# A macaron block on one core: x + y/2 scattered beside each row of f and added in its leaf tile

## The chip, the core and the metric

The kernel runs on one core of one Trainium2 chip. A core has a matrix engine (TensorE, PE in the profile; PEld is its weight load), a vector engine (VectorE, DVE), a scalar engine (ScalarE, ACT), a general engine (GpSimd, POOL) and a synchronising engine (SyncE, SP). Transfers between the core's memory (SBUF) and the chip's memory (DRAM) are issued from the queues of SP, ACT and POOL; those with a list of row numbers (indirect ones) are issued from POOL. PE's results land in a small memory of its own (PSUM, eight banks).

The metric is the time of one execution in microseconds (us) on the device, as the median of several runs. The profile comes from one profiled execution of the same program; its span reaches from its first to its last instruction.

## The reference

x has 4 x 1024 tokens of 256 values. The function does three steps; each adds to x:

```
x = x + 0.5 * ffn(layernorm(x))
x = x + attn(layernorm(x))          # 16 heads, latent k and v, rotation, masked by pages of 64
x = x + 0.5 * ffn(layernorm(x))
```

with the same ffn both times:

```
xn  = (x - mean) / sqrt(std + 1e-5)
q, k, v = tree_q(xn), tree_k(xn), tree_v(xn)             # relu inside
y   = xn + softmax(q k^T / sqrt(256)) v                  # over the 1024 tokens of a sequence
out = y + tree_f(y)                                      # gelu inside
```

A tree routes each token through eight levels of yes/no decisions (255 nodes) to one of 256 leaves. The leaf is a small two-layer network of its own: 256 to 16 values, an activation, 16 to 256.

So the second half of a step is x + 0.5 * (y + tree_f(y)), for every token.

## The kernel before

The 4096 tokens are 32 tiles of 128 (NT = 32). `xn` in SBUF holds a row of 256 values for each token, and in a 257th column, for the f tree, the token's number. `ffn` (line 1010) is called twice, with `attention` (line 1433) between; the text calls the two calls the first and the second pass.

A pass has these stages. First the norms and the routing of q, k and v. The tokens of a tree are sorted by groups of leaves into slots of 128-row tiles (at most 63 tiles, NGRP, of which mostly 48 to 53 are used), and `leaves` (line 810) runs the network of one such tile after another. Then comes the softmax stage: 32 steps, one for each tile of tokens. In step s, `begin_weights` transposes the exponentials of the tile before (PE L1001, copied out of PSUM by DVE and ACT at L1002), `score` makes the new scores (PE L978), their maximum (DVE L986) and the exponential (ACT L991), and `weigh` multiplies with v (PE L1006) and adds into `xn` (DVE L1008). That row of `xn` is now y. In the last eight steps the routing of f runs beside it (`route`: PE L389, L397, L409, DVE L405 and L417, POOL L419), then counting and ranking (`in_runs`, PE L455, L466, L467, L502, DVE L457 to L499), and the scatter of the rows of y to their slots in the DRAM buffer `xs_f` (`scatter`, POOL L691). Slots that get no token keep a row of zeros with a number that is out of bounds, written earlier by `clear` (ACT's queue, L329).

All of that stage stands in an order written out by hand: inside `in_order()` the engines PE, DVE, ACT and POOL run their instructions exactly as the program lists them. `at(step, where, do, ...)` puts a piece of work into a step: `where` 0 is ahead of the step's scores, 1 is between the scores' maximum and the exponential (and ahead of the routing's next piece), 2 is at the step's end. SP's queue takes its transfers in the order of the program, each waiting for what it depends on.

Then `leaves` runs for f. For each tile, SP loads 128 rows of `xs_f` (L820), PE transposes and multiplies them, DVE makes the masks, and at the end DVE adds the tile's rows of y to the result (L919), and POOL scatters the sum by token number into the DRAM buffer `ytok` (L920). The loads run four tiles ahead. Tiles past 48 run in branches of their own (`spare_leaves`). Beside the leaves, `reload` brings the pass's input x back into `xn` (SP, L128 in the first pass and L1380 in the second), as `xn` is no longer needed for y.

What follows needs x + 0.5 * ytok. `arrive` (line 1423) loads a piece of `ytok` (L1427) and adds it to `xn` (DVE L1429). After the first pass the attention calls it tile by tile as it begins, after a run of filler matmuls on PE (L144); it then takes the moments (bn_stats, L337), the layernorm (L1568), the latent and q, k, v matmuls (L1575, L1583, L1589) and the rotation (DVE L1486, L1488, POOL L1491), and transposes the result (L1499). After the second pass an end stage calls `arrive` for eight groups of four tiles (GT = 4) and stores each group into the output (ACT's queue, L1416).

In the pool `raw` two buffers with the tag "raw" take the f tree's first weights as they are loaded (`load_part`); their last use is in step 23.

## Time and profile before

| | |
|---|---|
| median of 11 runs | 2476.49 us (2473.18 to 2483.84) |
| the profiled execution's own time | 2478.45 us |
| its span | 2476.7 us |
| PE, DVE, ACT, POOL busy | 89%, 58%, 44%, 33% of the span |
| mean granted clock of PE | 0.945 |
| softmax stage, steps 26 to 31, second pass | about 2274 to 2337 us |
| 24 scatters of y rows without a gap, second pass | 2288.75 to 2319.1 us |
| f leaves, second pass | about 2355 to 2445 us |
| end stage | 2448.5 to 2476.7 us |
| opening of the attention | about 834 to 860 us |

The timeline lists instructions in order of time: start, length, engine, line and operation, tiles written and read, and in brackets how long the engine was idle before and what ended that. Lines like "x8" are several instructions in a row. The chain that ended last follows the work back from the last instruction, each step to what released it. The windows give, for a stretch, its length, the busy time of PE, PEld, DVE, ACT and POOL (with the number of instructions), PE's granted clock, the share of the DMA engines' time and the GB/s moved.

### The profile page before, as it was taken

The numbers are of one execution on the slowest core, as the hardware profiler recorded it, in microseconds if no ns is written. First come the engines' busy times: TensorE is split into PE (matmuls) and PEld (weight loads), VectorE is DVE, ScalarE is ACT, GpSimd is POOL, SyncE is SP. The second block draws the span as 40 slices with busy tenths as digits, with TensorE's granted clock in tenths as the row PEclk, the third lists the DMA queues.
The fourth block names the chain that finished last, engine by engine and source line by source line (L and its number), as shares of the span: only waits on it lengthen the run. The fifth ranks groups of instructions, "written<-read, shape, count | busy, mean of one in ns | idle before, by whom it ended". The sixth has DMA issues, their size and how long they took to land. (4 is left out here: it accounts for less than half of the span.)

```text
span 2476.7 us, 43530 instructions
## 1 busy us (share of the span) xinstructions
PE 2193.9 (89%) x14205; PEld 1419.1 (57%) x14205; DVE 1441.7 (58%) x4744; ACT 1096.9 (44%) x2902; POOL 818.4 (33%) x1053
## 2 busy tenths in 40 slices
PE   4498988999988899999999999985889989999794
PEld 2387866676657644334344434334778866766483
DVE  6676744333356766666676667745757543334475
ACT  3255655233214225555555555553556552332142
POOL 4554555343255421101101100002545663431553
PEclk8699999999998889999999999998999999999997
DMA  9667665343165300000000000017667553531655
GB/s 328 194 221 237 175 180 146 117 140 122 42 196 156 117 1 1 1 1 1 1 18 1 1 14 14 10 60 265 186 176 222 163 166 105 153 115 37 201 163 164
DMA packets 201877, 285.42 MB, mean 115 GB/s; under 512 B 25129, under 2 KB 174522, under 8 KB 197536
## 3 DMA queue, kind: packets, MB, share of 16 engines
q1 hardware_dynamic: 105232, 112.83, 14.1%
q0 software_dynamic: 35552, 91.87, 13.2%
q10 hardware_dynamic: 60848, 77.62, 9.6%
q8 instruction: 132, 2.16, 0.4%
q14 instruction: 113, 0.93, 0.1%
HBM read 182.75 MB, written 104.32 MB: 116 GB/s over the span
## 5 line engine op out<-in xcount | busy, mean ns | idle before, releaser
L1622 DVE TENSOR_REDUCE mxh<-big 128x1 f32<-128x512 f32 (+3 forms) x768 | 393.3, 552 | 194.1 <-PE big L1614 191.9
L1658 ACT ACTIVATE pTh<-big 128x512 f32<-128x512 f32 (+3 forms) x768 | 341.1, 491 | 288.9 <-PE big L1614 264.6
L1614 PE MATMUL big<-kTh,qTh 32*128 32x512 f32 (+3 forms) x1536 | 401.6, 539 | 1.3 <-ACT kTh L1595 1.2
L1650 PE MATMUL big<-qTh,kTh 32*128 32x512 f32 (+3 forms) x1536 | 399.8, 536 | 1.9 <-ACT pTh L1658 1.6
L829 ACT COPY xgT<-sm 128x256 f32<-128x256 f32 x399 | 148.4, 373 | 285.7 <-PE sm L827 255.5
L978 PE MATMUL two<-kT,qT 128*128 128x512 f32 x512 | 234.8, 603 | 10.2 <-issue 8.6
L1650 PEld LDWEIGHTS big<-qTh,kTh 32*128 32x128 f32 x1536 | 143.6, 184 | 156.3 <-issue 126.7
L1006 PE MATMUL sm<-vb,pT 128*128 128x256 f32 x1024 | 232.6, 380 | 0.0
L1006 PEld LDWEIGHTS sm<-vb,pT 128*128 128x128 f32 x1024 | 189.8, 190 | 24.7 <-issue 1.0
L827 PE MATMUL sm<-ident,xg 128*128 128x128 f32 x774 | 156.3, 286 | 42.9 <-DMA xg<-rows_x,inv_v 14.4
L986 DVE TENSOR_REDUCE mx<-two 128x1 f32<-128x1024 f32 x64 | 78.3, 1224 | 195.8 <-PE two L978 195.8
L865 DVE SCALAR_TENSOR_TENSOR went<-sm,sides 128x14 bf16<-128x14 f32 x399 | 68.3, 171 | 171.7 <-PE sm L856 162.1
L1669 PE MATMUL sm<-pTh,vpad 128*32 128x512 f32 (+3 forms) x1536 | 165.0, 501 | 0.0
L1614 PEld LDWEIGHTS big<-kTh,qTh 32*128 32x128 f32 x1536 | 146.6, 185 | 20.1 <-issue 14.2
L978 PEld LDWEIGHTS two<-kT,qT 128*128 128x128 f32 x512 | 94.1, 193 | 107.9 <-issue 103.1
L929 ACT COPY og<-sm 128x256 f32<-128x256 f32 x298 | 111.0, 373 | 79.5 <-DMA os_q<-og 16.0
L802 POOL DMA_INDIRECT xg<-rows_x,inv_q x101 | 101.2, 1002 | 114.0 <-PE sm L895 51.2
L920 POOL DMA_INDIRECT ytok<-og,tok x101 | 99.3, 983 | 80.4 <-DVE went L865 69.3
L419 POOL TENSOR_TENSOR acc<-acc,oh 128x32 bf16<-128x32 bf16 (+1 forms) x128 | 41.4, 323 | 252.5 <-DVE oh L417 216.0
L880 DVE TENSOR_TENSOR hm<-sm,mask 128x128 f32<-128x128 f32 x399 | 115.3, 289 | 10.0
L903 ACT ACTIVATE hid<-sm 128x128 f32<-128x128 f32 x399 | 112.9, 283 | 12.4 <-PE sm L895 11.8
L827 PEld LDWEIGHTS sm<-ident,xg 128*128 128x128 f32 x774 | 83.1, 148 | 60.9 <-issue 16.3
(367 smaller groups left out, 4541.9 us busy)
## 6 DMA issues: line engine op xcount, KB each, us to landing
xs_f<-zero ACTq DMA_DIRECT2D x14, 1028.0 KB
xg<-xs_f SPq DMA_DIRECT2D x101, 128.5 KB
os_q<-og SPq DMA_DIRECT2D x101, 128.0 KB
os_v<-og SPq DMA_DIRECT2D x101, 128.0 KB
os_k<-og SPq DMA_DIRECT2D x96, 128.0 KB
xn<-in_x SPq DMA_DIRECT2D x16, 512.0 KB
raw_q<-in_q_w SPq DMA_DIRECT2D x8, 1024.0 KB
w_q<-in_q_w SPq DMA_DIRECT2D x2, 4096.0 KB
```

The costliest lines, as they stand in the source:

```text
L827: nc.tensor.transpose(pa[:, c, :], xg[:, c * P : (c + 1) * P], ident)
L829: nc.scalar.copy(xT, pa)
L880: nc.vector.tensor_tensor(hm.rearrange("p (e l) -> p e l", l=LW), ph[:, :P].rearrange(split, l=LW), bc(mask[:, 0], 2, LW), ALU.mult,)
L903: nc.scalar.activation(hid, pt[:, 0], func)
L929: nc.scalar.copy(og, po)
L978: nc.tensor.matmul(ps[:, n0 : n0 + 512], qT[:, c, i * P : (i + 1) * P], kT[:, c, n0 : n0 + 512], start=(c == 0), stop=(c == KC - 1),)
L1006: nc.tensor.matmul(po, pT[:, j, :], vb[:, j, :], start=(j == 0), stop=(j == TPB - 1))
L1614: matmul = nc.tensor.matmul(ps[:, :n], qT[r : r + HPAD, hg, i * P : (i + 1) * P], kT[r : r + HPAD, hg, n0 : n0 + n], start=True, stop=True,)
L1622: nc.vector.tensor_reduce(maxima(b, hg)[:, i, c, u : u + 1], ps[:, :n], AX.X, ALU.max)
L1650: matmul = nc.tensor.matmul(ps[:, off:], kT[r : r + HPAD, hg, j * P : (j + 1) * P], qT[r : r + HPAD, hg, qb * QN + off : (qb + 1) * QN], s ...
L1658: nc.scalar.activation(pT[:, u, off:], ps[:, off:], AF.Exp, scale=1.0 / math.sqrt(HD))
L1669: nc.tensor.matmul(acc[r : r + HPAD, off:], vpads[b % 2][:, j, 4 * hg + 2 * pair + u, :], pTs[pair][:, u, off:], start=(j == 0), stop=(j = ...
```

## The change

A row of `xs_f` becomes 2 x 256 + 1 values wide: y, the token's number, and x + y/2. These rows are put together in SBUF, in buffers of four tiles (`sums[c]`, c from 0 to 7): `rest_of(c)` loads x (from the input, or in the second pass from `xrd`) into the last 256 columns, and `whole(t)` adds half of y to them on DVE and copies y and the number on ACT. The buffers share the tag "raw" with the weights for even c, and have a tag "sum" for odd c, two buffers each, so that group c takes the buffer of group c - 4. `scatter` then writes whole rows. In the order by hand, groups 0 to 3 are loaded in steps 24 and 25 and put together in step 26, groups 4 and 5 are loaded at the end of step 27 and put together in step 28, groups 6 and 7 are loaded at the end of step 28 and put together in step 30 and after the loop.

In the leaves, the first 257 columns are loaded as before, and the last 256 in a transfer of their own (`xs`). The result is 0.5 times the leaf's output plus `xs`, and is scattered by token into the output in the second pass, and in the first into `xmid`, from which the attention loads straight into `xn`. `reload`, the addition in `arrive` and the end stage are gone. In the first pass `clear` also zeroes the new columns, as a transfer of its own.

```diff
-    xs_f = dram.tile([NSLOT, E + 1], F32, name="xs_f")
-    ytok = dram.tile([NTOK, E], F32, name="ytok")
+    XSW = 2 * E + 1
+    xs_f = dram.tile([NSLOT, XSW], F32, name="xs_f")
+    xmid = dram.tile([NTOK, E], F32, name="xmid")
...
-    def scatter(slot, rows, views, *ts):
+    def scatter(slot, rows, views, sums, *ts):
...
-                in_=xn[:, t, :],
+                in_=sums[t // GT][:, t % GT],
...
-        raw = pool.tile([P, P, LW], F32, name=f"raw_{FFFS[f]}{hf}{c}", tag="raw", bufs=bufs)
+        size = GT * XSW if f == 3 else P * LW
+        raw = pool.tile([P, size], F32, name=f"raw_{FFFS[f]}{hf}{c}", tag="raw", bufs=bufs)
+        raw = raw[:, : P * LW].rearrange("p (e l) -> p e l", l=LW)
...
-                nc.sync.dma_start(xg, xs_f[g * P : (g + 1) * P, :])
+                nc.sync.dma_start(xg, xs_f[g * P : (g + 1) * P, : E + 1])
...
                 nc.vector.tensor_copy(tok, xg[:, E:])
-                kept[g] = tok, xg
+                xs = pool.tile([P, E], F32, name="xs", tag="xs", bufs=6)
+                nc.sync.dma_start(xs, xs_f[g * P : (g + 1) * P, E + 1 :])
+                kept[g] = tok, xs
...
-                tok, xg = kept.pop(g)
-                nc.vector.tensor_tensor(og, po, xg[:, :E], ALU.add)
+                tok, xs = kept.pop(g)
+                nc.vector.scalar_tensor_tensor(og, po, 0.5, xs, ALU.mult, ALU.add)
...
+                sums = {}
+
+                def rest_of(c):
+
+                    lo = c * GT
+                    sums[c] = raw.tile([P, GT, XSW], F32, name=f"sum{c}", tag=("raw", "sum")[c % 2], bufs=2)
+                    rows = (
+                        a["x"][lo // TPB, lo % TPB * P : (lo % TPB + GT) * P, :] if first
+                        else xrd[lo * P : (lo + GT) * P]
+                    )
+                    nc.sync.dma_start(
+                        sums[c][:, :, E + 1 :], rows.rearrange("(i p) e -> p i e", p=P)
+                    )
+
+                def whole(t):
+
+                    row = sums[t // GT][:, t % GT]
+                    nc.vector.scalar_tensor_tensor(
+                        row[:, E + 1 :], xn[:, t, :E], 0.5, row[:, E + 1 :], ALU.mult, ALU.add
+                    )
+                    nc.scalar.copy(row[:, : E + 1], xn[:, t, :])
...
-                    clear(nc.scalar, xs_f[k * 8 * P : min((k + 1) * 8 * P, NSLOT)])
+                    rows = slice(k * 8 * P, min((k + 1) * 8 * P, NSLOT))
+                    clear(nc.scalar, xs_f[rows, : E + 1])
+                    if first:
+                        clear(nc.scalar, xs_f[rows, E + 1 :])
...
                 at(26, 2, place_run, 0, 1)
                 at(27, 0, place_run, 0, 2)
+                for c in range(4):
+                    at(24 + c // 2, c % 2, rest_of, c)
+                    for t in range(c * GT, (c + 1) * GT):
+                        at(26, c % 2 + 1 - c // 2, whole, t)
                 for step in range(27, 30):
                     t = 8 * (step - 27)
                     for where, ts in enumerate((range(t, t + 2), range(t + 2, t + 5), range(t + 5, t + 8))):
                         at(step, where, go, *ts)
+                    if step < 29:
+                        for c in range(2 * step - 50, 2 * step - 48):
+                            at(step, 2, rest_of, c)
+                            for t in range(c * GT, min((c + 1) * GT, RUNS[1])):
+                                at(step + 1, c % 2, whole, t)
+                for t in range(24, 30):
+                    at(30, 1 + t // 28, whole, t)
                 for step, where in ((28, 0), (28, 1), (29, 0), (29, 1)):
                     at(step, where, place_run, 0, 1)
...
                 place_run(1, 9)
+                for t in range(30, NT):
+                    whole(t)
                 path = route(rp, (3,), NT - 1, *hot_f, 1)
...
-            def reload():
...
-                    places = dram_disjoint_views(ytok, NGRP)
+                    places = dram_disjoint_views(
+                        out.rearrange("b t e -> (b t) e") if last else xmid, NGRP
+                    )
...
-                    with_steps(leaves(*what), (1, reload()))
+                    drain(leaves(*what))
...
-            if last:
-                with ExitStack() as fs:
-                    ep = stage(fs, "end", 3)
-                    for c in range(NT // GT):
-                        ts_ = slice(c * GT, (c + 1) * GT)
-                        drain(arrive(ep, c * GT, (c + 1) * GT, nc.sync))
-                        nc.scalar.dma_start(
...
-    def arrive(pool, lo, hi, queue, tag="y", bufs=None):
...
+    def arrive(lo, hi, queue):
+
+        queue.dma_start(
+            xn[:, lo:hi, :E], xmid[lo * P : hi * P, :].rearrange("(i p) e -> p i e", p=P)
+        )
         yield
-        nc.vector.scalar_tensor_tensor(
-            xn[:, ts_, :E], y, 0.5, xn[:, ts_, :E], ALU.mult, ALU.add
-        )
```

## The prediction

> **What bounds the kernel now.** I read the chain that ended last, then the two places the change works in (the softmax stage before the f leaves, the opening of the middle attention), by timeline and by windows.
>
> The chain that ended last (start, length, what; us):
>
> ```profile
> 2444.15 4.34 DMA ytok<-og,tok
> ...
> 2449.32 4.52 DMA y<-ytok
> ...
> 2471.03 1.23 DVE xn L1429
> ```
>
> See: the last result scatter has landed at 2448.49. Everything after it, up to the span's end at 2476.70, is the end stage: eight loads of ytok, an addition each, eight stores.
>
> The softmax stage of the second pass, timeline, engine by engine (start, length, engine, line; idle before it in brackets):
>
> ```profile
> 2278.24 1.23 DVE L986 TENSOR_REDUCE mx<-two 128x1 f32<-128x1024 f32 x1 [3.13 <-PE two L978]
> 2279.57 0.28 DVE L417 TENSOR_TENSOR oh<-sm,rights 128x128 bf16<-128x128 f32 x1
> ...
> 2284.23 0.69 DVE L1002 COPY pT<-sm 128x512 f32<-128x512 f32 x1
> ...
> 2288.44 1.22 DVE L986 TENSOR_REDUCE mx<-two 128x1 f32<-128x1024 f32 x1
> ```
>
> ```profile
> 2282.10 0.18 PE L455 MATMUL sm<-acc,ones 128*128 128x32 bf16 x1
> ...
> 2291.20 1.09 PE L1001 MATMUL sm<-ident,pr 128*128 128x128 f32 x8 [0.23 <-ACT pr L991]
> ...
> 2296.18 0.17 PE L502 MATMUL sm<-upto,tri 32*32 32x1 bf16 x1
> ...
> 2299.84 1.04 PE L1001 MATMUL sm<-ident,pr 128*128 128x128 f32 x8
> ...
> 2320.41 0.18 PE L455 MATMUL sm<-acc,ones 128*128 128x32 bf16 x1 [1.31 <-POOL acc L419]
> ```
>
> See: PE is the bound and hardly idles. DVE has idle holes of 3 us, but it runs in written order, and in step 27 (2282.3 to 2291.0) there is no hole: the reduction at 2288.44 follows the ranks at once, and PE already waits 0.23 us for the exponential behind it. POOL issues 24 scatters without a gap from 2288.75 to 2319.1, one per 1.275 us; PE's 1.31 us wait at L455 is for POOL's sum behind them.
>
> PE clock (windows: length, busy of PE, PEld, DVE, ACT, POOL, PEclk):
>
> ```profile
> 850.00:851.00 1.00, 0.00 (x0) 0.00 (x0) 1.00 (x4) 0.00 (x0) 0.00 (x0) 1.00 0.00 0
> 851.00:852.00 1.00, 0.00 (x0) 0.00 (x0) 0.69 (x4) 0.00 (x0) 0.65 (x1) 0.57 0.00 0
> 852.00:853.00 1.00, 0.87 (x4) 0.71 (x4) 0.89 (x4) 0.00 (x0) 0.08 (x1) 0.50 0.00 0
> ```
>
> See: after about 2 us of idle PE the clock fell to half here. After the longer idle before the second pass's leaves it stayed at 0.50 from 2355 to about 2360.
>
> **The change part by part.** All is set against the profiled execution: span 2476.70, its time 2478.45.
>
> *End stage gone.* The span then ends shortly after 2448.49. I allow 0.5 us for the close: 2476.70 - 2449.0 = **-27.7** (bounds -26.5 to -28.2).
>
> *Opening of the attention.* The 17 additions at L1429 vanish, and bn_stats reads what the DMA brought. PE's first real matmul follows the filler at 845.7 and stays there. Then DVE's order counts: the q rotation (L1486) ran at 850.45 behind an addition of 1.20 us, though its matmuls (L1583) ended at 848.16; ACT's latent copy ran at 848.39, held by a factor that DVE gave late. Freed of them, rotation and both transposes behind it come 2.2 us earlier. Later additions (853.26, 859.57) may give a little more: **-3** (from -0.5, if another engine holds the chain, to -6, if the clock dip above also goes).
>
> *Whole rows made early.* Per pass 32 DVE operations of 128x256 with an immediate scalar: L1429's single-tile form took 426 ns, about 455 from start to start. 32 ACT copies: between 373 ns (L829, from PSUM) and 589 ns (L1117, SBUF to SBUF with scale and bias). ACT is 26% busy here (24.92 of the 97 us from 2240); in step 26 twelve copies, even of 589, leave the exponential done at 2284.9, just when the delayed PE comes for it. Cost nothing; without that cover the four of step 28 cost 2.4.
>  - Step 26, middle slot: eight of them (3.6 us) stand between the reduction and L417. L417 moves to 2283.2, POOL's sum behind it (0.44 us later, 1.21 long) ends at 2284.85, and PE's L455 runs at 2284.9 instead of 2282.10: +2.8. L1001 and the whole next step are queued behind it.
>  - Step 26, last slot: L457 to L662 (1.5 us, from 2285.1), then four more (1.8): the pT copy at 2288.4 instead of 2284.23. From that copy to the reduction it is 4.2 us with no hole: 2292.6 instead of 2288.44. With no slack behind it, **+4.2** in all so far.
>  - Step 28, first slot: four more, on rows that are loaded into the buffer that scatters 0 to 3 read. Scatter 3 ended on POOL at 2293.60, now 2297.8. Landing: the last xs_f scatter's POOL span ended at 2351.09 and the loads behind it were issued at 2352.93, so 1.84; in the first pass 2.0. Twice the bytes: bounds +0 and +1.0 (one more scatter's worth at the 130 GB/s or so of these stretches), I take +0.3. Then SP issues the 512 KB load: the first y load took 3.5 us to its addition (2448.89 to 2452.39); beside scatters a reload issued at 2295.30 still moved data until 2299.9, some 4.7 to 5.7 with its receipt. I take 4.3: there at 2304.5. DVE is ready at 2296.8 and waits 7.7. Then 1.8 for the four, 0.2 casts, 0.9 for the small chain to `upto`: PE's L502, in order ahead of L1006, runs at 2307.4 instead of 2296.18: **+11.2** in all. Both the exponential (reduction 2307.4) and step 29 sit behind.
>  - PE idles some 7 us there, so it resumes at half clock, as after 2355: 4.8 us at 0.5 lose **2.4**: +13.6. The 1.3 us wait at L455 (2320.41) is used up: **+12.3**.
>  - POOL: scatters 8 and 10 start after DVE's delayed casts (group 5's load lands at 2309.6, its four end at 2311.4), so the run of 24 ends 10.2 later, 2.1 ahead of PE. Step 30's six fit into DVE's holes of 2.2 (before L1008) and 1.0 us (before L457).
>
> Bounds per pass: 8.6 (landing 1.84, load 3.5, no clock loss) to 14.4 (landing 3, load 5.7). A second clock loss, for the 2.8 us wait of step 26, is left out: the dip at 851 came in a string of waits, here one stands alone. Two passes: **+24.6**.
>
> The Trainium skill, "TensorE: Matmul & The Clock Gate", Part 1, says that the clock halves after an idle window of about 3.4 us and returns after about as long a busy one: a rule against this change, which puts a 7 us hole into a stage that had none. By its figure the hole costs an estimated 1.7 in place of 2.4 and the whole sum would be 1.4 lower; the row above it, half clock after some 2 us of idle, is stricter than the rule.
>
> *Scatters with 2052-byte rows.* No row of the trace has them. POOL's time lies between 0.97 us (same 128 rows; a plain POOL load with 512 rows took only 0.82 to issue, so bytes and row count move it little) and 1.94 (proportional to bytes). I take 0.97, the nearer row.
>
> *Handover to the leaves.* Rows 30 and 31 put 0.9 us of DVE before L405, where it idled 0.79: +0.1. The last four scatters come after the 4 MB weights have gone by (350 GB/s until 2347), so their double size costs only its landing, +0.3 to +0.5. **+0.6** per pass (0 to 2), **+1.2**.
>
> *Leaves.* Steady tile: 1.507 us (L919 from 819.63 to 821.13), DVE busy 1.44 with a hole of 0.11. The new og form lies between 0.42 (L919) and 0.485 (L1008, pointer scalar): covered by the hole. If not, 0.06 x 50 = 3 per pass. 101 loads of xs (0.32 us of SP each) replace 16 reloads; SP has 1.2 us free per tile, xg buffers free earlier, and DMA share is 0.55. Nothing.
>
> *Clears.* Eight more of 1 MB in the first pass, on ACT's queue (0.37 us issue each) in steps with DMA at 0.40: nothing, at most +2 by late gathers.
>
> Sum: -27.7 - 3 + 24.6 + 1.2 = **-4.9**, 2473.55 against 2478.45. The median of the runs shown, 2476.49, is 1.96 below the profiled one: **2471.6**.
>
> **The rivals.**
>  1. *The holes hold it.* The rows arrive in time or DVE's waits fall beside PE work; only step 26's order costs (4.2 - 1.3 per pass). For: DVE is 44% busy in this stage. Against: the load cannot start before scatter 3 has landed, one slot ahead of its reader. -27.7 - 3 + 5.8 + 1.2 = -23.7: 2453.
>  2. *Longer rows cost POOL* (slower). The 24 + 4 scatters of a pass stand in a row on POOL; e more for each adds 56 e over both passes, less 4 (POOL ends 2.1 ahead of PE per pass). It turns to a loss at e = 0.16 us, over 0.2% from 0.25; at 0.3 it gives 2484, at 0.97 2522. For: POOL writes these DMAs itself, and no row of this length is measured. Against: the 512-row load above.
>  3. *A deeper wait* (even or slower). The loads of groups 4 and 5 share the queues with scatters of 262 KB each 1.275 us (206 GB/s) and take 4 to 7 us longer, per pass: 2480 to 2486. For: the queues peaked at 446 GB/s in such a load, so 190 to 240 are left. Against: 512 KB at 190 are 2.8 us, inside my 4.3.
>
> **How the numbers follow.** A measurement of this kernel can tell about 0.2% (5 us) from no change. Forecast case 0.58: its bounds run from -17 (-28.2 - 6 + 17.2) to +6 (-26.5 - 0.5 + 28.8 + 4), 2459 to 2482; 0.32 of it below -5, 0.22 within, 0.04 above. Rival 1 0.20, all faster. Rival 2 0.12: 0.02 within, 0.10 slower. Rival 3 0.10: 0.03 and 0.07. Faster 0.52, same 0.27, slower 0.21. The range leaves out the lower half of rival 1 and the upper parts of 2 and 3: 2453 to 2484.
>
> **What would show it.** No y or out loads after the last scatter; span ending about 0.5 us after its landing. In the second softmax stage: L455 of step 26 waiting about 2.8 us for POOL's sum; L502 of step 28 waiting about 7 us, with DVE stopped by the load of the recycled rows, then PEclk 0.5; 24 scatters with two gaps, each still 0.97. The attention's q rotation at about 3 us after the first real matmul instead of 4.7. I am wrong if the DVE wait in step 28 is under 3 us (rival 1), if a scatter takes over 1.1 us on POOL (rival 2), or if leaves take longer than 1.51 us a tile.

## The result, and the profile after

| | before | changed |
|---|---|---|
| median | 2476.49 us | 2536.13 us (2528.92 to 2541.59, 8 runs) |
| ratio, with its 95% interval | | 1.0238 (1.0224 to 1.0251) |
| the profiled execution's own time | 2478.45 us | 2522.99 us |
| its span | 2476.7 us | 2521.1 us |
| mean granted clock of PE | 0.945 | 0.943 |

The change makes the kernel 2.4% slower. The forecast was 2471.6 us with a range up to 2484, and 0.21 for slower.

Line numbers after the change are a little higher: the routing's sum is L420, its matmul L456, the small chain's matmul L503, the scores' exponential L996, the transposes L1006, the weights' matmul L1011, the fetch of q and k L1196, the rows' addition on DVE L1250 and copy on ACT L1253, the result's addition L924.

The stages can be set against each other by events that both traces have: the start of DVE's reduction (the scores' maximum) in each step of a softmax stage, the first and the last scatter of a result, and so on. In us:

| stretch | before | changed | difference |
|---|---|---|---|
| start to step 0, first pass (q, k, v) | 439.2 | 433.7 | -5.6 |
| first pass, steps 8 to 24 | 151.2 | 182.1 | **+30.9** |
| first pass, steps 26 to 31 | 48.5 | 64.2 | **+15.7** |
| first pass, step 31 to the first f result | 37.7 | 39.6 | +2.0 |
| first pass, f leaves | 71.1 | 71.1 | +0.1 |
| last f result to the attention's 48th maximum | 102.2 | 100.9 | -1.2 |
| second pass, steps 0 to 26 | 233.5 | 237.6 | +4.1 |
| second pass, steps 26 to 31 | 48.6 | 63.8 | **+15.2** |
| second pass, step 31 to the first f result | 37.3 | 39.2 | +1.9 |
| second pass, f leaves | 80.1 | 81.0 | +1.0 |
| last scatter to the end of the span | 32.5 | 13.2 | **-19.3** |

With -0.2 from the stretches not shown these make, but for rounding, +44.5, the difference of the spans. This profiled execution of the changed kernel is one of its quick ones, 13 us under its median. A second one, from the run `after_again` below, has a span of 2535.8; there the first row is -0.8, steps 8 to 24 +28.2, steps 26 to 31 +20.9 and +15.7. So the -5.6 in front, where nothing was changed, is scatter between executions and no part of the effect (in the runs below that start as fast, this stretch takes 436.0 to 443.9 us).

**The softmax stage of the first pass.** PE's waits of 3.9 to 7.6 us on rows of k that are fetched from DRAM by slot, timeline of the changed kernel:

```profile
509.56 0.41 PE L1196 MATMUL sm<-ident,y_k 128*128 128x128 f32 x2 [3.85 <-DMA y_k<-os_k,slot_k]
552.33 0.66 PE L1196 MATMUL sm<-ident,y_k 128*128 128x128 f32 x2 [7.62 <-DMA y_k<-os_k,slot_k]
600.52 0.66 PE L1196 MATMUL sm<-ident,y_k 128*128 128x128 f32 x2 [4.22 <-DMA y_k<-os_k,slot_k]
643.29 0.66 PE L1196 MATMUL sm<-ident,y_k 128*128 128x128 f32 x2 [6.37 <-DMA y_k<-os_k,slot_k]
```

These four make 22.1 us. After each of them the trace's records of the clock show it at half for 3.0 to 6.0 us of work, 16.6 us in all, which is an estimated 8 us more; the two together are 30 of the 30.9 us. The sum of these waits over the whole kernel, from the list of PE's waits, before and after (total, times, longest):

```profile
PE sm L1191 <- DMA y_k<-os_k,slot_k: 0.9, 1, 0.9
```

```profile
PE sm L1196 <- DMA y_k<-os_k,slot_k: 26.4, 8, 7.6
```

Windows of the same part of the stage (columns as ahead of the prediction; the last two are the DMA share and GB/s), before and after:

```profile
556.00:576.00 20.00, 20.00 (x91) 12.94 (x90) 7.09 (x13) 5.92 (x11) 1.99 (x6) 1.00 0.35 114
596.00:616.00 20.00, 20.00 (x91) 12.89 (x90) 7.09 (x13) 5.92 (x11) 3.87 (x8) 1.00 0.21 69
```

```profile
556.00:576.00 20.00, 20.00 (x93) 13.49 (x92) 6.89 (x12) 6.89 (x13) 3.81 (x4) 1.00 0.63 120
596.00:616.00 20.00, 15.78 (x68) 12.19 (x67) 5.07 (x9) 6.21 (x12) 5.79 (x7) 0.83 0.67 163
```

The first pair is the one to look at: the queues moved 120 GB/s instead of 114, but were busy 0.63 of the time instead of 0.35. The transfers had become slower, not only more. The records of single transfers say which. A clear's packets of 1028 bytes took 53 ns in the mean before; after the change those of 1028 bytes took 78 and those of 1024 bytes 103, with the same median (48 and 53) and a long tail. One clear lasted 3.3 to 5.4 us before, the pair of a step 11 to 16 us after, longer than a step of 9.4 us, and a fetch that is issued in that time shares the queues with it. In the second pass no byte is added to the clears, yet their packets rose from 52 to 80 ns: there only the distance between rows is new.

**Steps 26 to 31**, second pass, changed kernel, timeline of PE and then of DVE:

```profile
2329.66 0.18 PE L456 MATMUL sm<-acc,ones 128*128 128x32 bf16 x1 [1.68 <-POOL acc L420]
...
2339.72 1.09 PE L1006 MATMUL sm<-ident,pr 128*128 128x128 f32 x8 [1.13 <-ACT pr L996]
...
2353.56 0.18 PE L503 MATMUL sm<-upto,tri 32*32 32x1 bf16 x1 [8.79 <-DVE total L499]
2353.67 5.62 PE L1011 MATMUL sm<-vb,pT 128*128 128x256 f32 x16
...
2379.10 0.18 PE L456 MATMUL sm<-acc,ones 128*128 128x32 bf16 x1 [0.71 <-POOL acc L420]
...
2381.77 0.16 PE L488 MATMUL sm<-ones,acc 128*32 128x1 bf16 x1 [1.50 <-DVE cnt L458]
```

```profile
2325.29 2.77 DVE L1250 SCALAR_TENSOR_TENSOR sum<-xn,sum 128x256 f32<-128x256 f32 x8
...
2351.37 1.43 DVE L1250 SCALAR_TENSOR_TENSOR sum<-xn,sum 128x256 f32<-128x256 f32 x4 [10.27 <-DMA sum<-xrd]
...
2357.54 1.44 DVE L1250 SCALAR_TENSOR_TENSOR sum<-xn,sum 128x256 f32<-128x256 f32 x4 [2.48 <-DMA sum<-xrd]
...
2380.86 0.76 DVE L1250 SCALAR_TENSOR_TENSOR sum<-xn,sum 128x256 f32<-128x256 f32 x2 [1.95 <-DMA xs_f<-sum,slot_f]
```

Both waits of the prediction are there, in their places: the eight additions ahead of the routing in step 26 (PE waits for POOL's sum), and DVE's stop at the rows that are loaded into a buffer that scatters still read, with PE's small chain (L503) behind it and the weights' matmul at 5.62 us instead of 3.72. Before, that matmul was

```profile
2296.28 3.72 PE L1006 MATMUL sm<-vb,pT 128*128 128x256 f32 x16
```

A third wait is new: in step 30 (from 2374.58) DVE stops again, at the last two recycled rows that it makes there, and PE's L488 waits behind it. Counted from step 26's maximum (2278.24 before, 2323.96 after), PE's events come later by 1.8 us at the first routing sum (L455, now L456), by 11.7 at the small chain of step 28 (L503), by 13.0 at the second routing sum and by 15.2 at the small chain of step 30 (2387.60). So the second of DVE's waits, 2.48 us, cost nothing of its own, and step 30 cost 2.2 us. In the first pass of `after_again` step 30's wait is 6.43 us long, and that step takes 18.1 us instead of 11.5, which is what its +20.9 has over +15.7.

The clock around that stop, windows of 1 us:

```profile
2347.00:2348.00 1.00, 0.00 (x0) 0.00 (x0) 0.00 (x0) 0.57 (x3) 0.73 (x1) 0.65 1.15 45
2348.00:2349.00 1.00, 0.00 (x0) 0.00 (x0) 0.00 (x0) 0.00 (x0) 0.00 (x0) 0.50 0.68 171
...
2356.00:2357.00 1.00, 1.00 (x4) 0.82 (x3) 0.00 (x0) 0.30 (x2) 0.00 (x0) 0.50 1.12 416
2357.00:2358.00 1.00, 1.00 (x5) 0.86 (x4) 0.46 (x2) 0.00 (x0) 0.00 (x0) 0.73 0.92 357
```

PE's last work ended at 2344.77. A mean of 0.65 in the window from 2347 is 0.3 us at full and 0.7 at half clock, so the clock fell about 2.5 us after PE had stopped, and by the same reckoning it came back at about 2357.5, 4.0 us after PE had started again. The Trainium skill, "TensorE: Matmul & The Clock Gate", Part 1, gives about 3.4 us for both; here the fall came earlier and the return later. One wait gives no threshold, though. At the four waits for y_k above, the fall came 3.4 to 5.2 us after PE had stopped and the return 3.0 to 6.0 us after it had started again, and at a wait of 3.87 us in `after_again` (it ended at 514.33) the clock did not fall at all. In every trace here all stretches at half clock, but for those cut off by its end, last whole multiples of 3.41 us, so it matters where in this grid a wait falls.

**The end.** The chain that ended last is now one piece:

```profile
2507.95 0.98 DMA out<-og,tok
```

It started 13.2 us before the end of the span. What fills those is not in the views of the profile, since they leave out semaphore and queue work; the trace's own records have it (start, ns, engine, instruction, line):

```
2507.945   984  POOL  DMA_INDIRECT  out<-og,tok  L925
...
2512.540  7745  POOL  DRAIN  L1883
```

Between the two stands an instruction of 2054 ns on POOL, `INC_SWDGE_SEM`; the two together are called POOL's close here. SP was through by 2513.1 and waits for POOL until 2520.3. The same DRAIN of 7745 ns is in the trace of before, at 2448.74, where the end stage's loads and stores ran beside it.

### The profile page after: what moved, and what is told of

The parts are those of the page before. It is cut to its first block, busy times and chain, and to the rows that moved or that the text cites. A ratio compares the mean times of both kernels' runs of the same rounds, so it can differ in the third digit from the quotient of the medians.

```text
span 2521.1 us, 43872 instructions
## 1 busy us (share of the span) xinstructions
PE 2210.4 (88%) x14205; PEld 1427.0 (57%) x14205; DVE 1444.6 (57%) x4791; ACT 1116.3 (44%) x2966; POOL 817.2 (32%) x1053
## 3 DMA queue, kind: packets, MB, share of 16 engines
q10 hardware_dynamic: 64816, 81.69, 12.6%
## 5 line engine op out<-in xcount | busy, mean ns | idle before, releaser
L1011 PE MATMUL sm<-vb,pT 128*128 128x256 f32 x1024 | 240.8, 390 | 0.0
L1011 PEld LDWEIGHTS sm<-vb,pT 128*128 128x128 f32 x1024 | 195.8, 196 | 27.0 <-issue 1.0
L983 PEld LDWEIGHTS two<-kT,qT 128*128 128x128 f32 x512 | 96.1, 197 | 113.4 <-issue 110.2
L805 POOL DMA_INDIRECT xg<-rows_x,inv_q x101 | 102.2, 1011 | 108.2 <-PE sm L900 51.1
L420 POOL TENSOR_TENSOR acc<-acc,oh 128x32 bf16<-128x32 bf16 (+1 forms) x128 | 41.4, 323 | 261.0 <-DVE oh L418 217.7
L908 ACT ACTIVATE hid<-sm 128x128 f32<-128x128 f32 x399 | 113.1, 283 | 12.4 <-PE sm L900 11.7
L830 PEld LDWEIGHTS sm<-ident,xg 128*128 128x128 f32 x774 | 82.9, 148 | 59.0 <-DMA xg<-xs_f 16.6
L805 POOL DMA_INDIRECT xg<-rows_x,inv_k x90 | 91.9, 1021 | 67.4 <-PE sm L900 46.8
```

The costliest lines, as they stand in the source:

```text
L805: nc.gpsimd.indirect_dma_start(out=xg, out_offset=None, in_=rows_x, in_offset=bass.IndirectOffsetOnAxis(ap=inv[:, g : g + 1], axis=0),)
L830: nc.tensor.transpose(pa[:, c, :], xg[:, c * P : (c + 1) * P], ident)
L908: nc.scalar.activation(hid, pt[:, 0], func)
L983: nc.tensor.matmul(ps[:, n0 : n0 + 512], qT[:, c, i * P : (i + 1) * P], kT[:, c, n0 : n0 + 512], start=(c == 0), stop=(c == KC - 1),)
L1011: nc.tensor.matmul(po, pT[:, j, :], vb[:, j, :], start=(j == 0), stop=(j == TPB - 1))
```

## The experiments

The runs were made on several chips of one kind, and on some of them the kernel before takes 2580 to 2600 us instead of 2477, so each ratio is against runs of before on the same chip, and stage times from the longer-running chips are compared with each other only. The trace of `twice`, whose time there was that of before, is the base for these. It is a rough one: with the clears in short pieces, steps 8 to 24 of the first pass take 154.6 (`full2`) and 157.5 us (`made_last`) on such chips, against 160.0 in `twice`.

### The changed kernel again

> The changed kernel itself, to set the next runs against on the same chip: the chip of the first four runs ran the kernel before in 2600 us instead of 2476, so that only what runs on one chip can be compared. Its loss against before should be 45 to 75 us here as well, with y_k waits of some 20 us in the first pass and the wait for the recycled buffer in both.

Measured: 2534.67 us, 1.0227 (1.0199 to 1.0256) of before; y_k waits of 27.9 us. `clear_rows`, `all_three` and `tail_sp` are set against the same runs of before.

### What makes the clears slow

Seven runs change only clears. Mean duration of a clear's packets in the first pass and the loss of steps 8 to 24, against before's 151.2 us or, where marked *, against 160.0 in `twice`:

| run | clears of the first pass | packets, ns | loss of steps 8 to 24 | ratio to before |
|---|---|---|---|---|
| before | 1 MB contiguous, every second step | 53 (1028 B) | 0 | 1 |
| changed | 2 MB as two half rows | 78, 103 (1028, 1024 B) | +30.9 | 1.0238 |
| `twice` | the same 1 MB two times | 53 (1028 B) | base* | 0.9986 (0.9966 to 1.0005) |
| `wide` | 1 MB contiguous, 1 MB strided scratch | 89 (1028 B) | +25.6* | 1.0091 (1.0055 to 1.0128) |
| `new_rows` | 1 MB contiguous, 1 MB contiguous scratch | 61 (1028 B) | +12.7 | 1.0034 (1.0016 to 1.0052) |
| `clear_whole` | 2 MB of whole rows, contiguous | 151 (2052 B) | +19.1* | 1.0184 (1.0143 to 1.0226) |
| `clear_rows` | half rows, eight neighbours in turn | 72, 118 | +33.4 | 1.0266 (1.0237 to 1.0296) |
| `paced` | 1 MB of whole rows, every step | 109 (2052 B) | +8.6 | 1.0126 (1.0098 to 1.0154) |
| `clear_fine` | 0.5 MB of whole rows, twice a step | 99 (2052 B) | +0.7 | 1.0127 (1.0093 to 1.0162) |

A packet of 2052 bytes takes 85 to 88 ns where nothing holds it up (the median).

`twice`, on the kernel before:

```diff
-                    clear(nc.scalar, xs_f[k * 8 * P : min((k + 1) * 8 * P, NSLOT)])
+                    for _ in range(1 + first):
+                        clear(nc.scalar, xs_f[k * 8 * P : min((k + 1) * 8 * P, NSLOT)])
```

> The kernel before, in which every clear of the first pass is done a second time, to the same contiguous rows: as many bytes and packets as the changed kernel clears, but nothing strided. Theory 'pitch' (a clear is slow because its rows of 1028 and 1024 bytes stand 2052 bytes apart): each clear lasts 3 to 6 us as before, PE waits under 6 us in sum for late gathers of y_k in the first pass's softmax stage, and the time is 0 to 5 us over before. Theory 'volume' (a second megabyte per step is too much, however it lies): 22 us of such waits as in the changed kernel, 20 to 30 us over before. Third possibility, neither (the loss of the first pass's softmax stage comes from something else in the change): no difference, here and in the next run.

`wide`, on the kernel before (`new_rows` is the same with a scratch buffer `more` of [NSLOT, E + 1], cleared whole):

```diff
+    wide = dram.tile([NSLOT, 2 * E + 1], F32, name="wide")
...
-                    clear(nc.scalar, xs_f[k * 8 * P : min((k + 1) * 8 * P, NSLOT)])
+                    rows = slice(k * 8 * P, min((k + 1) * 8 * P, NSLOT))
+                    clear(nc.scalar, xs_f[rows])
+                    if first:
+                        clear(nc.scalar, wide[rows, : E + 1])
```

> The kernel before, in which each clear of the first pass (contiguous, as before) is followed by a second one of 1028-byte rows that stand 2052 bytes apart in a scratch buffer that nobody reads. 'Pitch': half of the packets are the slow ones, the pair lasts 8 to 13 us, 12 to 25 us over before. 'Volume': the same as the run with contiguous clears done twice, 20 to 30 us over before in both. Neither: under 5 us over before.

> The kernel before, in which each clear of the first pass is followed by a second one, contiguous like the first, of 1028-byte rows in a scratch buffer that nobody reads. It differs from the run with every clear done twice in one thing, that the second megabyte goes to rows of its own, and from the run with the strided scratch rows in one thing, the pitch. Theory 'burst' (about the first half to one megabyte of fresh memory is written at 48 ns a packet, and what comes soon behind it at half that speed, wherever it lies; rewriting the same rows is free): the second clear's packets take 70 to 130 ns in the mean, the pair 10 to 15 us, and the time is 10 to 25 us over before. Rival 'pitch' (only rows in the 2052-byte layout are slow): both clears at 48 to 60 ns, 0 to 5 us over before.

`clear_whole`, on the changed kernel (`zw` is a row of 513 zeros, but for the number out of bounds):

```diff
-                    clear(nc.scalar, xs_f[rows, : E + 1])
-                    if first:
-                        clear(nc.scalar, xs_f[rows, E + 1 :])
+                    clear(nc.scalar, xs_f[rows], zw)
```

> The changed kernel, with whole rows of 2052 bytes cleared in one contiguous transfer in both passes; the first pass clears the same bytes as the changed kernel in half as many, larger packets, the second pass twice its bytes. 'Pitch': a clear of 2 MB lasts 8 us or less, the first pass's softmax stage loses under 8 us against before instead of 31, the second under 5 instead of 4: 20 to 28 us less than the changed kernel, 2508 to 2516. 'Volume': no gain in the first pass and a loss of 10 to 25 us in the second: 2546 to 2561.

`clear_rows`, on the changed kernel:

```diff
-    def clear(queue, rows):
+    def clear(queue, rows, order="(g p) c -> p g c"):
...
-            rows.rearrange("(g p) c -> p g c", p=P), bc(zero[:, :width], 1, n // P)
+            rows.rearrange(order, p=P), bc(zero[:, :width], 1, n // P)
...
-                    clear(nc.scalar, xs_f[rows, : E + 1])
+                    order = "(p g) c -> p g c"
+                    clear(nc.scalar, xs_f[rows, : E + 1], order)
                     if first:
-                        clear(nc.scalar, xs_f[rows, E + 1 :])
+                        clear(nc.scalar, xs_f[rows, E + 1 :], order)
```

> The changed kernel, in which a clear of xs_f writes eight neighbouring rows for each partition instead of rows that stand 128 rows apart: the same bytes, packets and sizes, every packet 2052 bytes behind the one before it instead of 262656. Theory 'stride' (the first four runs: contiguous whole rows were as slow as the half rows, the doubled clear with 131584 bytes between rows was not, so it is the distance from one packet to the next): packets of 1028 bytes at 48 to 60 ns in the mean instead of 78 to 80, the pair of a step in 6 to 9 us instead of 11 to 16, y_k waits under 6 us, 20 to 35 us less than the changed kernel on this chip. Rival 'footprint' (new megabytes are slow to write wherever they lie): packets as slow as before, within 5 us of the changed kernel.

What follows. Doubling the writes to the same rows costs nothing (`twice`). But the second clear of a step starts there only when the first has ended (at 524.5 after 522.9, say), as both write the same rows, so each is a burst of one megabyte; whether it is the same rows or the shorter burst that makes it free is not separated. A second strided megabyte, in a buffer that nobody reads and on a kernel otherwise unchanged, brings most of the loss and its y_k waits back (`wide`: +25.6 us, waits of 26.8), so the clears cause it, and nothing else in the change is needed.

But the "pitch" of my expectation was too narrow. Whole contiguous rows were little better in the first pass (+19.1, against +24.5 for the half rows in `later_whole` on that chip), and in the second, where they doubled the bytes, steps 0 to 26 took 26.4 us more than in `twice`: the expected gain was missed. A second contiguous megabyte in rows of its own, which follows the first at once, was slowed a little, to 61 ns in the mean of both, which neither theory of `new_rows` had; it lost 12.7 us in the trace and 8 by the ratio. And a distance of 2052 bytes between one packet of a partition and its next, instead of 262656, gained nothing: `clear_rows` missed its 20 to 35 us altogether. The Trainium skill, "DMA: Bandwidth & Descriptors", section "Latency and other measured facts", tells of HBM copies that slow down when the rows of a partition stand a large power of two apart, 2 MiB and more. The distance here, 512 bytes over a quarter MiB, is far smaller, and taking it away did not help, so this run does not show that case.

What the slow clears share is how they run. Cut into eighths, a clear of the changed kernel's second pass (2244.1 to 2250.2) has packet means of

```
47 47 52 72 82 114 85 132 ns
```

and one of `clear_whole` (2286.7 to 2300.5), of 2052-byte packets, 85 93 97 137 252 247 448 173. They begin at the speed of undisturbed packets and fall off behind the first quarter to three quarters of a megabyte. Hence the two runs with shorter clears. `paced`, and `clear_fine` in the same way with 32 pieces of two tiles, at (3 + k // 2, 2 * (k % 2)):

```diff
+                    rows = xs_f[k * 4 * P : min((k + 1) * 4 * P, NSLOT)]
+                    if first:
+                        clear(nc.scalar, rows, zw)
+                    else:
+                        clear(nc.scalar, rows[:, : E + 1])
...
-                for k in range(8):
-                    at(6 + 2 * k, 0, clear_some, k)
+                for k in range(16):
+                    at(6 + k, 0, clear_some, k)
```

> The changed kernel, with the same rows cleared in 16 pieces, one in each of steps 6 to 21, instead of 8 in every second step: in the first pass one contiguous megabyte of whole rows per step, in the second half a megabyte of strided half rows. 'Burst': pieces of this size stay mostly within what is written at full speed, packets of 2052 bytes take 88 to 105 ns in the mean (150 in the run with 2 MB at a time), y_k waits fall to 0 to 8 us, 20 to 28 us less than the changed kernel, a ratio to before of 1.011 to 1.015. Rival 'bytes per time' (the write rate of the stage as a whole is what the gathers suffer from): the ratio stays at 1.02 to 1.024.

> The changed kernel, with the same rows cleared in 32 pieces, two in each of steps 3 to 18: half a megabyte of whole rows each in the first pass, a quarter of half rows in the second. Theory 'burst' (a clear is slow only past its first half megabyte or so, and it is the long clear that holds up the gathers behind it): packets of 2052 bytes at 86 to 105 ns in the mean, first-pass steps 8 to 24 lose 0 to 6 us against the kernel before instead of 31, the second pass's 0 instead of 4: 26 to 34 us less than the changed kernel, a ratio to before of 1.009 to 1.013. Rival 'bytes per time': no better than 16 pieces, steps 8 to 24 lose 8 to 12 us, 1.012 to 1.016.

Measured: steps 8 to 24 of the first pass lose 8.6 and 0.7 us instead of 30.9, steps 0 to 26 of the second pass nothing in both. The strided half rows of the second pass, at the old pitch, take 51 and 49 ns when they come in short pieces, against 80 in the changed kernel. PE's waits, `clear_fine`:

```profile
PE sm L1196 <- DMA y_k<-os_k,slot_k: 1.4, 2, 0.9
```

So the loss goes with the length of one uninterrupted burst of writes, and with short bursts the whole term is gone. By the medians the two runs can't be told apart (both 1.013), by their traces `clear_fine` is the better by 8 us in that stretch. What stays open is why rows of 1028 bytes side by side take a burst of a megabyte nearly at the speed of its first packets and rows of 2052 bytes only a part of that, whether it matters that the rows were not written just before, and whether the row's length does (1028 and 2052 bytes both have 4 bytes over a power of two); no run separates these.

### Steps 26 to 31, one wait after another

`later_whole`, on the changed kernel:

```diff
-                                at(step + 1, c % 2, whole, t)
+                                at(step + 1 + c % 2, 2 - 2 * (c % 2), whole, t)
```

> The changed kernel, in which the rows of group 4 are made at the end of step 28 and those of group 5 at the start of step 29, one to two slots later than in the change, so that DVE comes to them when their load has landed. Theory 'the wait for the recycled buffer' : PE's wait of 8.8 us at the small chain's first matmul in step 28 goes, and with it the half clock behind it: 7 to 10 us less per pass, 2516 to 2522. Rival 'POOL's row of scatters' (the 24 scatters in their new order end the stage in any case): the wait moves to PE's matmul that needs POOL's sum in step 29, 0 to 4 us less in both passes together, 2532 to 2536. The clears are untouched: 31 us of loss in the first pass by both.

Measured on one of the longer-running chips, 1.0110 (1.0067 to 1.0153) of before; the changed kernel was not run there, but `clear_whole`, whose steps 26 to 31 are the change's, was. Those steps take 60.2 and 59.8 us per pass, against 67.0 and 64.6 in `clear_whole` and 55.1 and 55.0 in `twice`. So 5 to 7 us per pass of the expected 7 to 10, and DVE waits for the next load:

```profile
2461.64 1.43 DVE L1250 SCALAR_TENSOR_TENSOR sum<-xn,sum 128x256 f32<-128x256 f32 x4 [3.75 <-DMA sum<-xrd]
```

`all_three` adds to `later_whole` the clears of `clear_rows` and makes groups 0 to 3 one per step at the head of steps 23 to 26:

```diff
-                    at(24 + c // 2, c % 2, rest_of, c)
+                    at((24, 20, 24, 21)[c], c // 2, rest_of, c)
                     for t in range(c * GT, (c + 1) * GT):
-                        at(26, c % 2 + 1 - c // 2, whole, t)
+                        at((25, 23, 26, 24)[c], 0, whole, t)
```

> The changed kernel with the clears by neighbouring rows, with groups 0 to 3 made one group per step at the head of steps 23 to 26 (their loads in steps 20, 21 and 24), and with groups 4 and 5 made one to two slots later (as in the earlier run). If clears, the eight operations ahead of the routing in step 26 and the wait for the recycled buffer are the three things that the change loses in the softmax stages: 45 to 60 us less than the changed kernel, and 5 to 15 us less than the kernel before, since the end stage's 19 us remain as gain. If POOL's row of scatters or the loads set the stage anyway, it gains only what the clears give, 20 to 35 us, and stays over the kernel before.

Measured: 1.0193 (1.0162 to 1.0224); steps 26 to 31 take 61.5 and 57.5 us instead of the 69.4 and 64.3 of `after_again`. The 2.8 us of step 26 are gone (step 26 to 27 is 10.2 us as before), but with POOL no longer held up, its scatters follow each other without a gap, and the load of group 5 comes late in their midst:

```profile
2366.29 1.43 DVE L1250 SCALAR_TENSOR_TENSOR sum<-xn,sum 128x256 f32<-128x256 f32 x4 [10.17 <-DMA sum<-xrd]
```

It was issued at 2357.9, 6.7 us after the scatters that read its buffer were done on POOL (2351.2). A wait taken away at one place came back at the next.

`full` makes tiles 16 to 23 in memory that is dead by then, so that their loads wait for no scatter (`rest_dead` loads the last 256 columns of so many tiles into such memory; groups 0 to 3 are made as in `all_three`, the first pass's clears are those of `paced`, the second's stand in the attention):

```diff
+                at(25, 1, rest_dead, qTs[0], 16, 3)
+                at(25, 2, rest_dead, kTs[0], 19, 3)
+                at(27, 2, rest_dead, vbs[0], 22, 2)
+                for t in range(16, 24):
+                    at(28 + (t - 16) // 4, 0, whole, t)
```

> The changed kernel, with what the runs so far point to: first-pass clears as in the paced run, second-pass clears moved into the attention (beside its stores, where the DMA queues are empty); groups 0 to 3 made one per step at the head of steps 23 to 26; the rows of tiles 16 to 23 made in memory that the last sequence's queries, keys and values no longer need, so that their loads wait for no scatter. If clears, step 26's order and the recycled buffer are what the softmax stages lose, both keep step for step with the kernel before but for 0 to 8 us in all, and what remains is the end stage's gain of 19 less 4 to 6 at the handovers: 5 to 18 us under before, a ratio of 0.993 to 0.998. If the paced clears don't hold, it stays 10 to 20 us over before.

Measured: 1.0227 (1.0189 to 1.0265), a miss in sum, but steps 26 to 31 take 51.1 and 51.0 us, 2.6 and 2.4 over before: the order of step 26 and the recycled buffer are the 15 us, so far as these two stretches go. The rest was lost to two new waits. Six of the second pass's eight clears were not issued in the attention but between the first pass's leaf loads on SP's queue, which made those leaves 113.4 us long instead of 71.1:

```profile
849.51 0.37 SPq L330 DMA_DIRECT2D xs_f<-zero  x1
868.64 0.37 SPq L330 DMA_DIRECT2D xs_f<-zero  x1
```

And the f tree's last weights (L702), issued on ACT's queue, fill the dead memory and waited there for the scatters out of it, with ACT's copy for PE behind them; step 31 to the first result took 50.2 and 49.9 us instead of 37.7 and 37.3:

```profile
2404.71 0.40 ACTq L702 DMA_DIRECT2D w_f<-in_f_w  x1
2405.20 0.58 ACT L1007 COPY pT<-sm 128x512 f32<-128x512 f32 x1 [7.68 <-DMA xs_f<-vb,slot_f]
```

`full2` leaves the second pass's clears in their stage, in the pieces of `clear_fine`, and loads those weights from SP's queue:

```diff
-                    w2 = load_second(nc.scalar, wp, 3)
+                    w2 = load_second(nc.sync, wp, 3)
```

> The version of the run before with the two things mended that its trace shows as new waits: the second pass's clears stay in its softmax stage (there they had cost nothing once they were paced; moved, they were issued among the first pass's f leaves and made these 41 us longer), and the f tree's last weights are loaded from SP's queue, because from ACT's they stood ahead of ACT's copies and waited for scatters out of the memory that they fill (10 to 11 us per pass). Clears are in 32 pieces of half a megabyte, two per step in steps 3 to 18. If these were the only new waits: first-pass steps 8 to 24 lose 3 to 9 us against the kernel before, steps 26 to 31 lose 2 to 4 per pass, the handovers 2 to 5 per pass, the end gains 19: 0.996 to 1.003 of the kernel before. If the weights now come too late for the first leaf, 5 to 10 us more per pass: 1.004 to 1.010.

Measured: 1.0050 (1.0032 to 1.0069), on a longer-running chip: steps 26 to 31 at 54.4 and 56.8 us (55.1 and 55.0 in `twice`), the handovers at 46.9 and 42.9 (36.6 and 37.4). The steps were mended, the handover was not.

`early_dead` puts the tiles that are scattered first (0 to 5) into the dead memory, with the weights on ACT's queue again, and makes and scatters tiles 22 and 23 in step 30 (each entry: step, place, first tile, number of tiles, buffer):

```diff
+                    (19, 0, 10, 4, "sum"), (20, 0, 18, 4, "sum"), (24, 0, 0, 3, qTs[0]), (24, 1, 6, 4, "raw"),
+                    (24, 2, 3, 3, kTs[0]), (25, 1, 14, 4, "raw"),
+                    (28, 2, 22, 4, "raw"), (29, 0, 26, 4, "sum"), (29, 1, 30, 2, "raw"),
...
+                at(30, 0, go, 22, 23)
```

> The changed kernel with the clears in 32 pieces, and with the rows made in other places and in another order: tiles 0 to 5, which are scattered first, in the memory of the queries and keys that are no longer needed, tiles 6 to 21 in the four buffers, tiles 22 to 31 in these again, one step later than in the change; the last weights stay on ACT's queue. Theory 'the weights waited for the scatters out of the memory that they fill': these have landed two steps earlier, so the handovers lose 1 to 4 us per pass against the kernel before instead of 5 to 13; steps 8 to 24 lose 0 to 6 in the first pass, steps 26 to 31 lose 0 to 4 per pass, the end gains 19: a ratio of 0.992 to 1.000. Rival 'the last scatters land later' (twice the bytes per row, whatever the order): handovers 5 to 10 us per pass as in the last two versions, 1.000 to 1.006.

Measured: 1.0127 (1.0106 to 1.0148). The handovers lose 1.9 and 2.2 us instead of `full`'s 12.6. That is not the weights' wait alone: this run has a long stop in step 30, in which the queues can empty, and the next two runs, without it, lose 7 to 10 us at the handovers though their weights are issued as early. So the weights' wait was at most some 6 us of the 12.6. From step 26 to 29 both passes keep pace with before to within 0.1 us. Then DVE waits 12.7 us for a recycled row's load, POOL's sum is behind it, and PE behind that:

```profile
2368.04 1.33 POOL L420 TENSOR_TENSOR acc<-acc,oh 128x32 bf16<-128x32 bf16 x4 [18.16 <-DVE rs L1012]
```

`seven_recycled` puts tiles 14 to 16 into the memory of the dead values too, so that only tiles 25 to 31 recycle a buffer (against `early_dead`; the tiles between move up to suit):

```diff
-                    (19, 0, 10, 4, "sum"), (20, 0, 18, 4, "sum"), (24, 0, 0, 3, qTs[0]), (24, 1, 6, 4, "raw"),
-                    (24, 2, 3, 3, kTs[0]), (25, 1, 14, 4, "raw"),
-                    (28, 2, 22, 4, "raw"), (29, 0, 26, 4, "sum"), (29, 1, 30, 2, "raw"),
+                    (19, 0, 10, 4, "sum"), (20, 0, 21, 4, "sum"), (24, 0, 0, 3, qTs[0]), (24, 1, 6, 4, "raw"),
+                    (24, 2, 3, 3, kTs[0]), (25, 0, 17, 4, "raw"), (27, 0, 14, 3, vbs[0]),
+                    (28, 2, 25, 4, "raw"), (29, 0, 29, 3, "sum"),
```

`made_last` makes four of these seven in step 31 (against `seven_recycled`):

```diff
-                for t in range(25, 29):
-                    at(30, 1 + t // 28, whole, t)
+                for t in range(25, 29):
+                    at(31, t // 28, whole, t)
...
-                at(30, 2, go, *range(RUNS[1], RUNS[2]))
+                at(30, 2, go, RUNS[1])
+                at(31, 0, go, *range(RUNS[1] + 1, RUNS[2]))
```

> The run before with early rows in dead memory, in which the rows of tiles 14 to 16 stand in the memory of the values that are no longer needed, so that only tiles 25 to 31 use recycled buffers, and no scatter ahead of POOL's sum in step 30 waits for a load. Theory 'loads into recycled rows': steps 26 to 31 keep within 0 to 4 us per pass of the kernel before, clears cost 0 to 2, the handovers 2 to 3 per pass, the end gains 19: a ratio of 0.992 to 0.998. Rival 'backlog' (the scatters of doubled rows fill the queues so long that whatever is loaded behind them, the last weights and the first leaf's rows too, comes late): steps 26 to 31 and the handovers lose 10 to 20 us per pass together, 1.002 to 1.010.

> The run before with seven recycled rows, in which these are made in step 31 instead of step 30 and scattered in step 31, but for one. Theory 'loads into recycled rows': the wait in step 30 goes and nothing takes its place, 12 to 16 us less, a ratio of 0.996 to 1.001. Rival 'backlog': the step 30 wait goes, but the first leaf's rows come no sooner, because they wait for the landing of all scatters; the handover loses 10 to 14 us per pass against the kernel before instead of 5 to 7, and the ratio stays at 1.003 to 1.007.

Measured: `seven_recycled` 1.0062 (1.0040 to 1.0084), its steps 26 to 31 56.4 and 55.3 us with one wait left,

```profile
2341.92 0.19 PE L456 MATMUL sm<-acc,ones 128*128 128x32 bf16 x1 [7.71 <-POOL acc L420]
```

and handovers 6.7 and 8.4 us over before. `made_last` 1.0048 (1.0025 to 1.0070): that wait is gone (54.0 and 54.3 us, 55.1 and 55.0 in `twice`), and the handovers take 46.1 and 45.7 us, 9.6 and 8.3 more than in `twice`. The rival "backlog" was right: PE stands idle at the first leaf in any case.

```profile
2472.47 1.25 PE L830 MATMUL sm<-ident,xg 128*128 128x128 f32 x4 [12.57 <-DMA xg<-xs_f]
```

The scatters' own packets show why (second pass). Before, 28 scatters of 32 packets of 4112 bytes take 168 to 193 ns a packet, as means of eighths, and the last packet ends 1.1 us after POOL's last issue (2331.3 to 2330.2). In `made_last` they are 64 packets of 4104 bytes each; the first six scatters (1.6 MB) run at 168 to 170 ns, those behind them at 395 in the mean and up to 787, and the last packet ends 14.3 us after the last issue (2453.5 to 2439.2). In the changed kernel the packets kept to 160 to 181 ns for 17 scatters (4.5 MB) and ended 10.1 us after the issue: there DVE's waits had put gaps of 4 to 5 us between the scatters. It is the pattern of the clears again: without waits, the doubled rows are issued faster than they are written.

What this does to the handover: the f tree's last weights come beside and behind these packets, and the last four scatters beside the weights. Counted from step 31's maximum, the weights' packets end at 21.0 us before and at 35.4 in `made_last`, the last scatter's at 25.4 and 33.3, and the first leaf's load is issued behind that, at 26.1 and 34.4.

### The end

`tail_sp`, on the changed kernel:

```diff
+                if out_rows:
+                    n = g % NT
+                    nc.sync.dma_start(out_rows[0][n * P : (n + 1) * P], og)
+                else:
                     nc.gpsimd.indirect_dma_start(
```

> The changed kernel, in which the results of the second pass go out in the order of their slots, as plain stores from SP's queue, so that POOL has nothing to issue in these leaves; the scatter of the results by token is left out. Theory 'POOL's close' (the changed kernel ends 13 us after the start of its last scatter because POOL closes its queue only behind it, 2.1 and 7.7 us): the span ends 3 to 6 us after the last addition instead of 13 to 14, 6 to 10 us less. Rival 'landing' (the last transfer's landing takes that long however it is issued): 0 to 3 us less.

Measured, with two executions: from the start of the last addition to the end of the span 6.2 us instead of 14.8 (2527.26 to 2533.4; in `after_again` 2521.01 to 2535.8), so the exposed close is 8.6 us. In sum nothing was gained, 1.0256 (1.0220 to 1.0293): from the first addition to the last these leaves take 87.8 us instead of 79.7. The plain stores stand in SP's queue among the loads of the leaves, and DVE waits 10.2 us in all for stores to free the result's buffers and 5.6 for rows of the next tiles. The mechanism is shown; as a remedy it is none.

No version tried beats the kernel before; the nearest are `made_last` and `full2` at 1.005.

## Why the prediction was wrong

**Failed: "Clears ... nothing, at most +2 by late gathers".** They cost 30.9 us in the first pass and 4.1 in the second, 35 of the 49 us between the forecast for the profiled execution (2473.55) and what it took (2522.99). I priced the clears by their issue on ACT and by the mean DMA share of the stage. Neither says how long one transfer occupies the queues, nor what a fetch issued meanwhile waits. And I counted bytes only, so that the second pass, whose clears keep their bytes but not their layout, was not looked at. `wide` and `clear_fine` show the term, by bringing it into the kernel before and by taking it out of the changed one. "Late gathers" named the right wait, at under a tenth of its size; that the clock falls behind such waits was not thought of.

**Mis-sized: the end stage, -27.7 with "0.5 us for the close".** It was -19.3. The scatters' landing was right, but the close is POOL's, 2.1 and 7.7 us, which the end stage had covered. The trace of before had the 7.7 us, and the list of chains does not show it because queue work is not counted there. My bounds (-26.5 to -28.2) excluded it for no reason that the profile gave.

**Right in place, low in size: whole rows made early, +12.3 per pass.** It was +15.7 and +15.2, over the bound of 14.4. Step 26 cost 1.8 us at L455 and 2.8 by the next maximum, where I had 2.8 and 4.2. DVE's wait in step 28 was 10.3 us instead of 7.7: DVE came 1.4 us sooner, and the rows 1.2 later, since the load was issued 3.4 us after scatter 3's end on POOL and then took 5.3 (2.4 and 4.3 in my sum). PE's small chain was late by 11.7 us, where I had 11.2. The clock loss was 1.9 us at L1011 against 2.4. The 1.3 us stall at L455 in the end did not give itself up wholly (0.7 us remain). That makes 13.0; the other 2.2 came in step 30, whose six additions I had let fit into DVE's holes. `full` confirms the causes together by taking them away: 2.4 to 2.6 us are left.

**Wrong in mechanism: opening of the attention, -3.** It was -1.2, inside the bounds (-0.5 to -6), but that is luck. The q rotation was to come about 3 us after the first real matmul instead of 4.7; it came 6.6 us after it (894.80 after 888.17), because DVE ran the statistics of later tiles (L338, L339) ahead of it. And the difference is no more than scatter: the same stretch takes 99.2 us in `new_rows`, where it is unchanged, and 100.0 to 104.3 in the runs with the change that start as fast as before.

**Mis-sized: handover, +0.6 per pass.** It was +2.0 and +1.9, at the bound, and +2.7 to +5.8 in `after_again`, `paced` and `clear_fine`, where it is the same code. `made_last` shows what stands behind it: twice the bytes behind 28 scatters, which in the changed kernel the other waits partly hid.

**Right: leaves at nothing** (+0.1 and +1.0), **and scatters at 0.97 us on POOL.** Rival 2 is false as I put it, as POOL took 0.97 to 1.01 us each. What the rows cost came out in the queues instead, 13 to 14 us behind POOL's last issue once the other waits were gone. The Trainium skill, "Perfetto Trace Analysis", section "DMA Instruction — SWDGE (GPSIMD)", says that the profile's end of such an instruction is when its descriptors are written, not when the data is moved; these runs agree, and I should have asked about the landing of all 28 and not only of the last. Rival 1 is false, since the wait in step 28 is over 3 us. Rival 3 had a deeper wait in the right place, at a fraction of the loss.

With all terms as measured the forecast's own sum is -19.3 (end) - 1.2 (opening) + 30.9 (whole rows) + 3.9 (handovers) + 35.0 (clears) + 1.0 (leaves) = +50.3, of which the profiled execution shows +44.5, since it ran 5.6 us ahead before the first changed instruction.

## What to carry to other kernels

A transfer that nobody waits for is not free: price its duration in the queues, packet by packet, against the deadline of the fetches that are issued while it runs, and ask this of every transfer whose layout changes, even if its bytes do not. Long writes to DRAM are better cut into pieces of half a megabyte or less and spread over the steps; that alone took 27 to 30 us out of the first pass here. When a closing stage is removed, look in the trace's records for what ran under it, POOL's close above all. And when waits are taken away one after another, compare the sum: here each one gone let the doubled writes pile up sooner, and at the last 18 us stood in the handovers, which had lost 4 at first.

## What the runs showed that I had not expected

- Writes to rows of the 2052-byte layout start at 21 to 24 bytes per ns and packet and fall off within one burst: packets of 2052 bytes at 85 ns in the first eighth and 173 to 448 in the last ones (`clear_whole`), scatter packets of 4104 bytes at 169 ns for 1.6 MB and then up to 787 (`made_last`). Contiguous rows of 1028 bytes written twice, one megabyte after the other, showed no such fall (53 ns, `twice`).
- The layout of the rows matters beside the amount: two contiguous megabytes in rows of 1028 bytes took 61 ns per 1028 bytes, one megabyte at a pitch of 2052 bytes 80. Why was not found; a smaller distance between successive packets of a partition did not help (`clear_rows`).
- POOL's last DRAIN takes 7745 ns, with an `INC_SWDGE_SEM` of 2054 ns ahead of it, in the changed kernel, in its repeat and in the kernel before; the two are in none of the profile's sums.
- All stretches at half clock, but for those cut off by the end of the trace, last whole multiples of 3.41 us. In the changed kernel's softmax stages the clock fell 2.5 to 5.2 us after PE had stopped for a long wait, and returned after 3.0 to 6.0 us of work.
